# Keeping one over the norms in PSUM, and a second buffer for the rotary product, in the local-attention transformers

## The chip, the core and the metric

The program runs on one core of one Trainium2 chip. The metric is the device time of one execution in microseconds. Three executions of the kernel before took 4264.73, 4267.34 and 4271.99 us, so their median is 4267.34 us. Engines are called PE (matrix), DVE (vector), ACT (scalar activations), POOL (GpSimd) and SP (the queue that issues most transfers).

## The reference, cut to what matters

The whole computation is a chain of four stages. Each stage normalises `x`, runs one branch `s` and one branch `g`, and adds `s * silu(g)` to `x`. The change touches two of the `g` branches: stacks of local-attention transformer layers, one of six layers (16 heads, window 32) and one of two layers (8 heads, window 64). What is computed there for queries and keys is:

```python
def l2norm(t):
    return t / jnp.maximum(jnp.linalg.norm(t, axis=-1, keepdims=True), 1e-12)

qkv = x @ Wqkv
q, k, v = jnp.split(qkv, 3, -1)
q = l2norm(q) * qs
k = l2norm(k) * ksc
q = q * cos * scale + rotate_half(q) * sin * scale
k = k * cos * inv + rotate_half(k) * sin * inv      # inv = 1.0 / scale
out = local_attention(q, k, v)
return out @ Wo
```

Rotation and scaling commute with the division by the norm, so the kernel rotates first and divides last.

## The kernel before, in words

Everything is float32 with channels on the 128 partitions and the 512 positions of one batch on the free axis; there are four batches. The first 1600 us are three earlier stages. Then `transformer("l2")` runs from about 1600 us to 3640 us of the profiled execution, a recurrence follows, and `transformer("l3")` runs from about 3790 us to 4180 us.

In a transformer, a row is one layer of one batch. A row of l2 is cut into two halves of its heads, so l2 has 24 rows and 48 slots, and l3 has 8 rows and 8 slots. `merge` interleaves three Python generators within a slot by weights written by hand:

- `queries_keys` makes the queries and keys of one slot. For queries (i = 0) and keys (i = 1) and for two groups g it runs two projections on PE into a PSUM tile `S`, squares them on ACT (L1287, tile `sqp`), adds the two halves of the squares on POOL (L1288), multiplies the projections by the cosine table on DVE (L1289, into `l_rot`) and by the sine table on DVE (L1291, into `rotp`), and adds the two on POOL (L1292, into `l_rot`).
- `unit_length`, called once for the queries and once for the keys of a slot (96 calls in l2, 16 in l3), sums the squares over the channels with two matmuls of 128x512 into another `S` tile. ACT makes one over the norm out of it in two steps, the logarithm (L1312) and the exponential of minus half of it (L1313), into an SBUF tile `rn`. DVE then multiplies `l_rot` by it in two instructions of 128x1024 (L1316), one for each group. Eight transfers issued on SP's queue (L1323) move the result into the layout of attention (`l_qk`).
- `attention` works on the slot before: values (L1344 copies them out of PSUM, L1346 and L1348 move them), scores (L1377 on PE, L1387, L1391, L1396, L1398 for the softmax), transposes (L1412, L1461) and the output product.
- `feed_forward` of an older row is spread over two slots in l2. In the text, a slot of kind A holds its layer norm (matmuls with `hb,l_k` and `ffg,core`, ACT L1515, L1519, L1520), and a slot of kind B its three gelu tiles (matmuls with `hb,l_w`, ACT L1532, DVE L1534).

[...]A transformer's pool `ps` has three buffers of two banks for all tiles named `S`, and its pool `pm` two of one bank for the tiles named `M`. Projections, sums of squares, values, scores, transposes and feed-forward tiles all take their `S` tile from those three buffers. SBUF tiles of `unit_length` and `queries_keys` come from the pool `t`: `rn` and `rotp` have one buffer each, `sqp` three, `l_rot` two.

The order of the instructions on each engine, and which of the three PSUM buffers a tile gets, are not written by hand: a scheduler decides both when the program is built, from the generators' order and its own durations. The order on each engine is then fixed. A tile that is held longer thus changes which buffers other tiles get.

Of the kernel before, what the change touches and what calls it, by code (L numbers as in the profile page):

```python
# [16 lines left out]
F32 = mybir.dt.float32  # L17
BF16 = mybir.dt.bfloat16
AF = mybir.ActivationFunctionType
ALU = mybir.AluOpType  # L20
# [4 lines left out]
B, S, D = 4, 512, 128  # L25
# [1143 lines left out]
class _Transformer:  # L1169
# [93 lines left out]
    def queries_keys(self, rows):  # L1263


        net, nc, W = self.net, self.nc, self.W
        for l, b in rows:
            hb = net.shifted(net.tok(self.y, b), self.TP, 3)

            hk = hb.rearrange("p (u s k) -> p s u k", s=2, k=W)  # L1270
            for gp in range(self.GP):
                w = self.part("qk", l, gp)
                before = None
                made = []
                for i in range(2):
                    tab = self.tables(l, i)
                    t = self.TP.tile([128, 2, 2, S], F32, name=self.pre + "_rot", bufs=2)
                    sums = []
                    for g in range(2):
                        p = self.S2()  # L1280
                        for h in range(2):
                            c = 128 * (4 * g + 2 * i + h)
                            o = p[:, h, :]
                            net.mm(o.rearrange("p (s u k) -> p s u k", s=2, k=W) if i else o, w[:, c : c + 128], hk if i else hb)
                            yield 0.86
                        sq = self.TP.tile([128, 2, S], F32, name="sqp", bufs=3)
                        nc.scalar.activation(sq, p, AF.Square)  # L1287
                        nc.gpsimd.tensor_tensor(sq[:, 0, :], sq[:, 0, :], sq[:, 1, :], ALU.add)  # L1288
                        nc.vector.tensor_tensor(t[:, g], p, tab[:, 0], ALU.mult)  # L1289
                        m = self.TP.tile([128, 2, S], F32, name="rotp", bufs=1)  # L1290
                        nc.vector.tensor_tensor(m, p, tab[:, 1], ALU.mult)  # L1291
                        nc.gpsimd.tensor_tensor(t[:, g], t[:, g], m[:, ::-1, :], ALU.add)  # L1292
                        sums.append(sq)
                        if before:
                            made.append((yield from self.unit_length(*before)))
                            before = None
                    before = sums, t
                made.append((yield from self.unit_length(*before)))
                self.made[l, b, gp] = hb, made
                yield None  # L1300

    def unit_length(self, sums, t):

        net, nc = self.net, self.nc
        p = self.S2()
        for g in range(2):
            net.mm(p[:, g, :], self.ones, sums[g][:, 0, :])
            yield 0.86  # L1310
        rn = self.TP.tile([128, 2, S], F32, name="rn", bufs=1)
        nc.scalar.activation(rn, p, AF.Ln, bias=self.tiny)  # L1312
        nc.scalar.activation(rn, rn, AF.Exp, scale=-0.5)  # L1313
        for g in range(2):

            nc.vector.scalar_tensor_tensor(  # L1316
                t[:, g], rn[:, g, :].unsqueeze(1).to_broadcast([128, 2, S]), 1e12, t[:, g], ALU.min, ALU.mult
            )
        out = self.QK.tile([128, 2, 2, S], F32, name=self.pre + "_qk")
        for r in range(4):  # L1320
            for h in range(2):
                x = 32 * (2 * (r % 2) + h)
                nc.sync.dma_start(out[x : x + 32, :, r // 2, :], t[32 * r : 32 * r + 32, :, h, :])  # L1323
        return out
# [365 lines left out]
```

## Time and the profile before

| | |
|---|---|
| median of three runs | 4267.34 us (4264.73 to 4271.99) |
| the profiled execution, its own time | 4258.36 us |
| its span, first to last instruction | 4256.7 us |
| mean granted clock of PE | 0.927 |
| PE busy in l2 (1600 to 3640 us) | 1737.69 of 2040 us |
| DVE busy in l2 | 1435.78 us |
| ACT busy in l2 | 918.42 us |
| POOL busy in l2 | 742.16 us |
| L1316, 224 instructions, whole program | 366.2 us busy, mean 1672 ns |

A row of the profile names the line of the kernel, the engine, the operation, and the tiles as output <- inputs. The tile names `l2_rot` and `l3_rot` are both shown as `l_rot`. "Idle before" is the time that an engine stood idle before such an instruction, and the name behind the arrow is what ended that idle time. Busy shares are averages; what a change in one instruction is worth depends on who waits for it.

### The profile page before, as it was taken

The numbers are of one execution on the slowest core, as the hardware profiler recorded it, in microseconds if no ns is written. First come the engines' busy times: TensorE is split into PE (matmuls) and PEld (weight loads), VectorE is DVE, ScalarE is ACT, GpSimd is POOL, SyncE is SP. The second block draws the span as 40 slices with busy tenths as digits, with TensorE's granted clock in tenths as the row PEclk, the third lists the DMA queues.
The fourth block names the chain that finished last, engine by engine and source line by source line (L and its number), as shares of the span: only waits on it lengthen the run. The fifth ranks groups of instructions, "written<-read, shape, count | busy, mean of one in ns | idle before, by whom it ended". The sixth has DMA issues, their size and how long they took to land.

```text
span 4256.7 us, 105246 instructions
## 1 busy us (share of the span) xinstructions
PE 3632.9 (85%) x46765; PEld 1894.8 (45%) x46891; DVE 2521.8 (59%) x3429; ACT 1832.3 (43%) x2495; POOL 1200.4 (28%) x994
## 2 busy tenths in 40 slices
PE   7887999898999986888888888888888888768888
PEld 4554555344444433444444444444444444334444
DVE  6665555205433516677677777777667676447775
ACT  3344666331333343444444444444444444424554
POOL 1011444100111224333333433343333333033221
PEclk7678999996989988999999999999999999879999
DMA  1000000000000004334233424333333332222221
GB/s 35 7 24 26 1 1 1 28 10 7 1 3 2 1 15 113 85 81 106 70 89 98 95 67 120 70 86 94 86 73 92 87 85 69 75 85 68 58 63 43
DMA packets 123574, 236.11 MB, mean 55 GB/s; under 512 B 29625, under 2 KB 44129, under 8 KB 117729
## 3 DMA queue, kind: packets, MB, share of 16 engines
q1 hardware_dynamic: 114064, 209.58, 20.3%
q10 hardware_dynamic: 8624, 19.29, 1.4%
q8 instruction: 369, 6.05, 0.6%
q0 software_dynamic: 432, 0.51, 0.1%
q14 instruction: 85, 0.69, 0.1%
HBM read 50.08 MB, written 5.54 MB: 13 GB/s over the span
## 4 chain that ended last, share of the span: by engine, by line
PE 53%; DVE 16%; ACT 16%; issue 8%; POOL 3%; DMA 3%; SPq 1%; DVEq 0%; POOLq 0%; ACTq 0%
PE S L122 29%; PE M L122 8%; PE S L126 4%; PE S L1377 3%; PE o L1092 3%; DVE l_rot L1316 3%; DVE rotp L1291 3%; ACT l_P L581 3%; DVE l_rot L1289 2%; ACT l_PT L1412 2%; PE o L614 2%; ACT rn L1312 2%; POOL l_rot L1292 2%; ACT sqp L1287 1%; ACT l_P L1396 1%
## 5 line engine op out<-in xcount | busy, mean ns | idle before, releaser
L1292 POOL TENSOR_TENSOR l_rot<-l_rot,rotp 128x1024 f32<-128x1024 f32 x224 | 533.3, 2381 | 459.1 <-DVE rotp L1291 421.6
L1288 POOL TENSOR_TENSOR sqp<-sqp 128x512 f32<-128x512 f32 x224 | 315.6, 1410 | 1010.2 <-ACT sqp L1287 1009.6
L122 PE MATMUL S<-hb,l_wqk 128*128 128x512 f32 x896 | 501.4, 659 | 108.4 <-ACT l_vo L1344 32.3
L1287 ACT ACTIVATE sqp<-S 128x1024 f32<-128x1024 f32 x224 | 229.3, 1024 | 411.0 <-PE S L122 408.6
L1316 DVE SCALAR_TENSOR_TENSOR l_rot<-rn,l_rot 128x1024 f32<-128x1024 f32 x224 | 366.2, 1672 | 64.8 <-ACT rn L1313 62.3
L1289 DVE TENSOR_TENSOR l_rot<-S,l_tab 128x1024 f32<-128x1024 f32 x224 | 272.9, 1218 | 163.7 <-ACT sqp L1287 161.8
L126 PE MATMUL S<-core,l_P 128*128 128x128 f32 x1856 | 269.5, 288 | 57.3 <-DVE rotp L1291 13.5
L122 PE MATMUL S<-l_KT,l_QT 32*128 32x256 f32 (+7 forms) x1536 | 261.9, 505 | 34.8 <-ACT l_P L1114 14.2
L126 PEld LDWEIGHTS S<-core,l_P 128*128 128x128 f32 x1856 | 211.3, 146 | 177.2 <-issue 67.4
L1291 DVE TENSOR_TENSOR rotp<-S,l_tab 128x1024 f32<-128x1024 f32 x224 | 271.6, 1213 | 22.0 <-POOL l_rot L1292 21.8
L122 PE MATMUL S<-sqp,l_k 128*128 128x512 f32 x448 | 241.7, 633 | 33.3 <-POOL sqp L1288 24.9
L1114 ACT ACTIVATE l_P<-S 128x1024 f32<-128x1024 f32 x160 | 156.7, 1022 | 254.6 <-PE S L122 254.5
L1377 PE MATMUL S<-l_qk 64*32 64x64 f32 (+1 forms) x13312 | 222.1, 236 | 43.3 <-issue 34.3
L122 PEld LDWEIGHTS S<-hb,l_wqk 128*128 128x128 f32 x896 | 150.1, 199 | 244.0 <-issue 102.2
L122 PE MATMUL S<-l_wv,hb 128*64 128x256 f32 (+1 forms) x1600 | 237.1, 403 | 7.8 <-ACT rn L1312 2.4
L1377 PEld LDWEIGHTS S<-l_qk 64*32 64x32 f32 (+1 forms) x13312 | 174.1, 110 | 154.5 <-issue 151.0
L1412 ACT COPY l_PT<-S 128x1024 f32<-128x1024 f32 x128 | 129.5, 1012 | 250.1 <-PE S L126 250.0
L1067 DVE TENSOR_REDUCE l_mx<-S 128x2 f32<-128x768 f32 (+1 forms) x192 | 154.9, 863 | 134.1 <-PE S L1006 134.1
L1398 DVE TENSOR_REDUCE rs<-l_P 128x16 f32<-128x1024 f32 (+1 forms) x128 | 155.8, 1217 | 124.2 <-ACT l_P L1396 124.1
L122 PE MATMUL M<-l_OT,l_wo 128*128 128x512 f32 (+1 forms) x512 | 222.7, 546 | 4.1 <-ACT l_OT L1461 2.2
L1118 POOL TENSOR_SCALAR_AFFINE_SELECT l_P<-l_P 128x256 f32<-128x256 f32 x256 | 99.4, 406 | 409.9 <-ACT l_P L1114 405.1
L1387 DVE TENSOR_REDUCE mx<-S 128x16 f32<-128x1024 f32 (+1 forms) x128 | 155.7, 1217 | 98.7 <-PE S L1377 98.5
(359 smaller groups left out, 6619.9 us busy)
## 6 DMA issues: line engine op xcount, KB each, us to landing
l_qk<-l_rot SPq DMA_DIRECT2D x896, 128.0 KB
l_ve<-l_vo SPq DMA_DIRECT2D x112, 256.0 KB
l_ve<-l_vo SPq DMA_DIRECT2D x96, 224.0 KB
l_tab<-in_k_rot_l ACTq DMA_DIRECT2D x16, 1024.0 KB
l_wqk<-in_l2Wqkv SPq DMA_DIRECT2D x12, 512.0 KB
l_wv<-in_l2Wqkv SPq DMA_DIRECT2D x12, 256.0 KB
l_wo<-in_l2Wo SPq DMA_DIRECT2D x12, 256.0 KB
l_ve<-l_vo SPq DMA_DIRECT2D x24, 128.0 KB
```

What stands on the lines that cost most here:

```text
L122: self.nc.tensor.matmul(out, lhsT, rhs, start=start, stop=stop)
L126: self.nc.tensor.transpose(out, in_, self.ident[:n, :n])
L1114: nc.scalar.activation(P[u], s[u], AF.Exp, scale=scale)
L1287: nc.scalar.activation(sq, p, AF.Square)
L1288: nc.gpsimd.tensor_tensor(sq[:, 0, :], sq[:, 0, :], sq[:, 1, :], ALU.add)
L1289: nc.vector.tensor_tensor(t[:, g], p, tab[:, 0], ALU.mult)
L1291: nc.vector.tensor_tensor(m, p, tab[:, 1], ALU.mult)
L1292: nc.gpsimd.tensor_tensor(t[:, g], t[:, g], m[:, ::-1, :], ALU.add)
L1316: nc.vector.scalar_tensor_tensor(t[:, g], rn[:, g, :].unsqueeze(1).to_broadcast([128, 2, S]), 1e12, t[:, g], ALU.min, ALU.mult)
L1377: net.nc.tensor.matmul(sv[W * bl : W * bl + W, e, t, g, :].rearrange("p (s k) -> p s k", s=2), qk[0][r, g, j, W * c : W * c + W], kw, star ...
L1398: nc.vector.tensor_reduce(rs, P.rearrange("p t g e k -> p (t g e) k"), axis=AX.X, op=ALU.add)
L1412: self.nc.scalar.copy(u["PT"], t)
```

## The change

The tile `rn` is gone. The logarithm and the exponential are written back into the PSUM tile `p` that holds the sums of squares, and the two divisions on DVE read one over the norms there. So this `S` tile is given back after the second division instead of after the logarithm. The tile `rotp` gets a second buffer in SBUF; it is as large as `rn` was, 4 KB in each partition.

```diff
-                        m = self.TP.tile([128, 2, S], F32, name="rotp", bufs=1)
+                        m = self.TP.tile([128, 2, S], F32, name="rotp", bufs=2)
...
-        rn = self.TP.tile([128, 2, S], F32, name="rn", bufs=1)
-        nc.scalar.activation(rn, p, AF.Ln, bias=self.tiny)
-        nc.scalar.activation(rn, rn, AF.Exp, scale=-0.5)
+        nc.scalar.activation(p, p, AF.Ln, bias=self.tiny)
+        nc.scalar.activation(p, p, AF.Exp, scale=-0.5)
         for g in range(2):
 
             nc.vector.scalar_tensor_tensor(
-                t[:, g], rn[:, g, :].unsqueeze(1).to_broadcast([128, 2, S]), 1e12, t[:, g], ALU.min, ALU.mult
+                t[:, g], p[:, g, :].unsqueeze(1).to_broadcast([128, 2, S]), 1e12, t[:, g], ALU.min, ALU.mult
             )
```

No instruction is added or taken away. Line numbers behind L1310 are lower by one after the change.

## The prediction

> **What bounds the kernel now.** I read the page's engine rows first, then the stretch of l2 alone, then the lines that change, then who PE waits for, then one slot in order of time.
>
> ```profile
> 1600.00:3640.00 2040.00, 1737.69 (x29203) 888.16 (x29296) 1435.78 (x1528) 918.42 (x1034) 742.16 (x434) 0.97 0.36 87
> ```
> The columns are PE, PE's weight loads, DVE, ACT, POOL, clock, DMA share and GB/s. In l2, PE is busy 85% of the time and stands idle for 302 us. Those 302 us are nearly all that a faster DVE can buy there. l3 (3790 to 4180 us) has 63 us of PE idle time.
>
> ```profile
> L1288 POOL TENSOR_TENSOR sqp<-sqp 128x512 f32<-128x512 f32 x224 | 315.6, 1410 | 1010.2 <-ACT sqp L1287 1009.6
> L1316 DVE SCALAR_TENSOR_TENSOR l_rot<-rn,l_rot 128x1024 f32<-128x1024 f32 x224 | 366.2, 1672 | 64.8 <-ACT rn L1313 62.3
> ```
> The page's groups: count, then busy us and mean ns of one, then idle time before. L1316's instructions one by one, beside two others of their size (shortest, median, longest ns):
> ```profile
> L1316 DVE SCALAR_TENSOR_TENSOR l_rot<-rn,l_rot x224: 1207/1226/3368, 1622.9 to 4175.8; 128x1024 f32<-128x1024 f32 x112
> L1289 DVE TENSOR_TENSOR l_rot<-S,l_tab x224: 1171/1223/1226, 1610.6 to 4168.5; 128x1024 f32<-128x1024 f32 x112
> L1291 DVE TENSOR_TENSOR rotp<-S,l_tab x224: 1172/1214/1226, 1611.7 to 4170.9; 128x1024 f32<-128x1024 f32 x112
> ```
> The size is equal and the operands differ: L1289 and L1291 read one operand in PSUM and are never longer than 1226 ns; L1316 reads two in SBUF and reaches 3368 ns.
>
> ```profile
> PE S L122 <- issue: 60.6, 37, 4.5
> PE S L126 <- ACT l_PT L1412: 45.1, 44, 1.1
> PE S L122 <- DVE rotp L1291: 42.5, 40, 7.1
> PE S L122 <- ACT l_vo L1344: 36.7, 47, 1.1
> PE S L1377 <- issue: 30.5, 38, 4.1
> PE S L126 <- DVE rotp L1291: 23.4, 31, 5.0
> ...
> PE S L122 <- ACT rn L1312: 1.4, 2, 1.2
> ```
> These are PE's waits in l2: total us, times, longest. 66 us end with L1291, which stands behind L1316 in DVE's queue. Only 1.4 us end with the logarithm L1312, which releases the sums' buffer today.
>
> ```profile
> 2513.47 1.21 DVE L1291 TENSOR_TENSOR rotp<-S,l_tab 128x1024 f32<-128x1024 f32 x1
> 2515.91 4.50 DVE L1316 SCALAR_TENSOR_TENSOR l_rot<-rn,l_rot 128x1024 f32<-128x1024 f32 x2 [1.22 <-ACT rn L1313]
> 2521.22 0.69 DVE L1521 TENSOR_TENSOR hb<-S,ffu 128x512 f32<-128x512 f32 x1 [0.81 <-ACT ffu L1520]
> ...
> 2514.77 2.35 POOL L1292 TENSOR_TENSOR l_rot<-l_rot,rotp 128x1024 f32<-128x1024 f32 x1 [2.31 <-DVE rotp L1291]
> 2517.08 2.25 POOL L1288 TENSOR_TENSOR sqp<-sqp 128x512 f32<-128x512 f32 x1
> ```
> One slot of kind A in order of time (start, us). While POOL works, two divisions take 4.50 us and POOL's add 2.25; alone (2505.14) the pair took 2.36, and L1288's usual time is 1.27. Over l2 the pairs span 2.45 and 4.42 us (queries, keys of kind A) and 3.48 and 3.22 (kind B).
>
> **The change part by part.**
>
> *Divisions.* 224 at 1226 in place of 1672 ns free 100 us of DVE; L1288 at its median 1272 in place of 1410 frees 31 us of POOL. No row shows this instruction with an operand in PSUM. Bounds: 1223 ns (L1289) and 1672 (still stretched); I take 1223. [...]
>
> *Logarithm and exponential.* 112 of each as before. No row writes PSUM from ACT. Bounds for the exponential: 1022 ns (L1114, PSUM to SBUF, the nearest), and 2.1 us if reading and writing one bank took turns (twice 1058). I take 1.06 us: 0.
>
> *The buffer held longer.* Before, a sums' tile is held from its first matmul to the end of L1312, 4.86 us in the median; to the end of the second division of the same call it would be 10.2. With the old choice of buffers, the next tile in that buffer starts before that division's end in 74 of 96 calls of l2 and 12 of 16 of l3, by 318 and 48 us in sum. [...]But the changed program's order shows that the scheduler hands buffers out anew. PE's work (0.86 us for each 128x512 product, 0.11 for a 128x256 one, 0.03 for a small one, as spaced in the trace) between the sums and the next tile of that buffer is then 7.2 or 9.7 us for the queries (next are the keys' sums), and for the keys 2.6 in kind A (next is `hb,l_k`) and 4.3 in kind B (`hb,l_w`). Needed are 1.11 + 1.06 + 2.35 and four hand-overs of 0.04 to 0.1, about 4.75. So queries wait for nothing, and kind A's keys stall PE by 2.1 us.
>
> *What that stall is worth* I walk through in the slot above, in the changed order. Keys' sums end 2513.63, logarithm 2514.78, exponential 2515.87, divisions 2518.25 instead of 2520.41. PE: projections to 2515.66, eight value products to 2516.5, then the stall; `hb,l_k` 2518.3 to 2519.3; eight value products to 2520.2; `ffg,core` to 2521.15. ACT copies the values by 2521.3, and the masks, at 2521.96 before, start at 2521.3: before, PE stood waiting there for ACT's copies anyway. Behind the divisions on DVE are now the two copies L89 and L90, which wait for those value products, then L1289 and L1291, done 2523.5 (before 2524.99). The next projections need that buffer: 2523.5 (before 2522.92). Transposes L126 of `l_P` 2524.5 (before 2525.05), of `l_On` 2526.6 (before 2527.62). Scores follow, and behind them `mx` L1387, earlier by 2 us if PE's stream doesn't stall as it did before (2.46 us, "issue", at 2530.4 to 2533.03), by about 0.5 if it does. I take 1.2 us gained for kind A. The same walk through kind B (2541 to 2583 us): `hb,l_w` now waits for a value copy in its own buffer (2559.2 instead of 2557.01), the three gelu tiles end 2564.7 (before 2564.9), masks 2566.25 (before 2566.74), transposes of `l_On` about 2571 (before 2572.37), values held by L1291 at 2574.4 (before 2574.94): 0.5 us gained.
>
> *SP and transfers.* Eight transfers of `l_qk` start with the divisions' end, so 2.2 us sooner in kind A; PE waits for them 0.4 us in all, and POOL's L1292 35.8 us in 14 places, off the path: 0. The transfers of the values queue behind them on SP; were those on the path, up to 2 us more for each slot of kind A.
>
> *Second `rotp`.* L1291 waited 21.8 us for POOL's add in 22 places. Gain between 0 and 21.8; part lies in the walk, so 5 more. It lets POOL fall behind by one add; POOL is busy 36%, which hides it.
>
> *Sum.* 22 pairs of slots at 1.7: -37. Four slots of l2 without feed-forward have 3.4 us of cover against 4.75: +4. l3: cover 4.8 for the keys, but there the division starts 2.46 us behind the logarithm, so 5.9 are needed: 8 x 1.2 = +9. `rotp` -5. Total -29, say -30: the profiled execution, 4258.36 us, becomes 4228. It stands 9 us under the median of 4267.34; the forecast for the median is 4237.
>
> **The rivals.**
>
> *DVE is the limit more than the walk shows.* All the stretch comes off the path: 2.0 + 1.1 + 0.8 us for each pair, 24 pairs, -94; 4173. For: 66 us of PE wait end with L1291. Against: much of PE's waiting is ACT's copies and "issue", which stay.
>
> *PE's own stream decides.* The stalls named "issue" (60.6 + 30.5 us, no cause shown) and ACT's copies absorb what DVE gains: 0; 4267.
>
> *Slower: the held buffer binds.* Place: the third tile after the keys' sums, `hb,l_k` in kind A and `hb,l_w` in kind B. Price: 4.75 less the cover, 2.15 + 0.45, if nothing behind it comes back: 24 x 2.6 = 62, with l3 +71, less 10 for `rotp`; 4328. With a part recovered, 4300. It decides from the point where the stall is more than the 2 us by which the divisions shorten, for instance where other DVE work stands in front of them or the exponential takes over 2 us.
>
> *It doesn't do what it says.* The division stays stretched in PSUM too: the walk's 2520.45 in place of 2518.25 turns kind A into +1.5; 24 x 1.5 = 36; 4303. Against: 448 rows of L1289 and L1291 with no stretch.
>
> **How the numbers follow.** The forecast -30 has 0.45 (its own range 4207 to 4259), the large gain 0.17, nothing 0.12, the held buffer 0.21, the stretch that stays 0.05. A measurement of this kernel tells about 0.2%, 8.5 us, from no change. Faster: 0.45 + 0.17 = 0.62; same 0.12; slower 0.26. The range 4182 to 4312 leaves out half of the large gain and the worse half of the held buffer.
>
> **What the changed profile would show.** Right: L1315 (the division) at 1223 ns with no long ones, 275 us in all; L1288 near 1272; the exponential's row (L1312 then) at 1.02 to 1.12 us; L1291 no longer waiting for POOL; a new wait of PE on L1315 of about 2 us in every second slot of l2; PE's waits on L1291 down from 66 us. Wrong: L1315 with a longest time over 2 us, an exponential near 2 us, PE's waits on L1315 over 100 us in sum, or PE's waits in l2 not smaller than 302 us.

## The result, and the profile after

The changed kernel took 4201.92 us in the median of 4 runs (4199.46 to 4212.01). The kernel before took 4266.03 us beside it (4259.58 to 4271.99). The ratio is 0.9854, with a 95% interval of 0.9833 to 0.9876: 64 us less, where 30 us less was forecast. The profiled executions are 55 us apart (4203.18 against 4258.36 us), since that of the kernel before was 8 us under its median; the sums below are made against these 55.

The first view is the table of busy time in a stretch of l2. Columns are PE, PE's weight loads, DVE, ACT, POOL, granted clock, DMA share and GB/s.

```profile
1600.00:3600.00 2000.00, 1721.69 (x29476) 896.95 (x29571) 1368.06 (x1536) 913.36 (x1036) 711.34 (x434) 0.98 0.37 91
```

PE is busy in 86% of this stretch instead of 85, and DVE in 68% instead of 70. PE therefore still has idle time of 278 us in 2000. The kernel did not come to the end of what PE can give.

Next the rows of the instructions that change. The first two are groups of the page (count, busy us, mean ns, idle before), the others rows of single lines (shortest, median and longest ns), the last two of them of the kernel before:

```profile
L1315 DVE SCALAR_TENSOR_TENSOR l_rot<-S,l_rot 128x1024 f32<-128x1024 f32 x224 | 267.1, 1220 | 86.4 <-ACT S L1312 76.6
L1288 POOL TENSOR_TENSOR sqp<-sqp 128x512 f32<-128x512 f32 x224 | 287.4, 1283 | 856.8 <-ACT sqp L1287 856.5
L1315 DVE SCALAR_TENSOR_TENSOR l_rot<-S,l_rot x224: 1206/1223/1226, 1627.8 to 4123.1; 128x1024 f32<-128x1024 f32 x112
L1311 ACT ACTIVATE S<-S,l_tiny x112: 1068/1088/1097, 1623.1 to 4119.8; 128x1024 f32<-128x1024 f32 x112
L1312 ACT ACTIVATE S<-S x112: 1008/1008/1046, 1624.2 to 4120.9; 128x1024 f32<-128x1024 f32 x112
```
```profile
L1312 ACT ACTIVATE rn<-S,l_tiny x112: 1096/1114/1138, 1616.8 to 4172.5; 128x1024 f32<-128x1024 f32 x112
L1313 ACT ACTIVATE rn<-rn x112: 1055/1058/1088, 1617.9 to 4173.6; 128x1024 f32<-128x1024 f32 x112
```

The division's longest time fell from 3368 to 1226 ns and its mean from 1672 to 1220. POOL's L1288 came down with it, from 1410 to 1283. The logarithm and the exponential, now both in place in PSUM, are 26 and 50 ns shorter, not longer.

PE's waits in the same stretch of l2 (total us, times, longest):

```profile
PE S L122 <- DVE rotp L1291: 76.4, 77, 7.2
PE S L122 <- ACT l_vo L1343: 41.6, 52, 1.1
PE S L122 <- issue: 28.2, 31, 2.1
PE S L1376 <- issue: 23.4, 32, 4.2
PE S L122 <- DVE l_rot L1315: 21.0, 21, 1.0
PE S L126 <- DVE rotp L1291: 15.8, 33, 2.4
...
PE S L126 <- ACT l_PT L1411: 11.3, 43, 1.1
```

The new wait is the row on L1315: 21 times 1.0 us, once for nearly every slot of kind A. Gone are 34 us on `l_PT`, and 32 us of the "issue" before L122. Waits on L1291 had been forecast to fall; they went from 66 to 92 us.

Measured from logarithm to logarithm, the time went as follows (queries' logarithm of a slot to that of the next, one profiled execution each; a steady slot is the mean of 21 or 22, and single ones lie up to 5 us from it):

| part | before | after | difference |
|---|---|---|---|
| up to l2's first logarithm | 1616.8 | 1623.1 | +6.3 |
| l2, first four slots (no feed-forward) | 165.3 | 151.4 | -13.9 |
| l2, one steady slot of kind B | 42.30 | 40.91 | -1.39 |
| l2, one steady slot of kind A | 42.96 | 42.41 | -0.55 |
| l2, all 48 slots | 2010.7 | 1954.6 | -56.1 |
| between l2's last and l3's first logarithm | 169.0 | 166.6 | -2.4 |
| l3, first to last logarithm | 376.0 | 375.5 | -0.5 |
| after l3's last logarithm | 84.2 | 81.7 | -2.5 |

The parts sum to the 55 us. The 6.3 us at the start go with one wait of PE for the weights of the first projection, 6.8 us.

### The profile page after: what moved, and what is told of

Same layout as the page of the kernel before. It is cut to its first block, busy times and chain, and to the rows that moved or that the text cites. A ratio compares the mean times of both kernels' runs of the same rounds, so it can differ in the third digit from the quotient of the medians.

```text
span 4201.5 us, 105470 instructions
## 1 busy us (share of the span) xinstructions
PE 3603.6 (86%) x46765; PEld 1896.5 (45%) x46891; DVE 2439.9 (58%) x3429; ACT 1824.6 (43%) x2495; POOL 1166.3 (28%) x994
## 4 chain that ended last, share of the span: by engine, by line
PE 50%; DVE 20%; ACT 16%; issue 7%; DMA 3%; POOL 3%; SPq 1%; DVEq 0%; POOLq 0%; ACTq 0%
PE S L122 27%; PE M L122 8%; PE S L126 4%; DVE l_rot L1289 4%; DVE rotp L1291 4%; PE o L1092 3%; ACT l_P L581 3%; ACT sqp L1287 2%; DVE l_rot L1315 2%; PE S L1376 2%; PE o L614 2%; ACT l_PT L1411 1%; ACT l_vo L1343 1%; POOL l_rot L1292 1%; ACT l_P L1395 1%
## 5 line engine op out<-in xcount | busy, mean ns | idle before, releaser
L1292 POOL TENSOR_TENSOR l_rot<-l_rot,rotp 128x1024 f32<-128x1024 f32 x224 | 532.6, 2379 | 417.3 <-DVE rotp L1291 395.2
L122 PE MATMUL S<-hb,l_wqk 128*128 128x512 f32 x896 | 489.0, 646 | 93.0 <-DVE rotp L1291 39.0
L1288 POOL TENSOR_TENSOR sqp<-sqp 128x512 f32<-128x512 f32 x224 | 287.4, 1283 | 856.8 <-ACT sqp L1287 856.5
L1289 DVE TENSOR_TENSOR l_rot<-S,l_tab 128x1024 f32<-128x1024 f32 x224 | 272.9, 1218 | 216.7 <-ACT sqp L1287 215.1
L1287 ACT ACTIVATE sqp<-S 128x1024 f32<-128x1024 f32 x224 | 229.7, 1025 | 298.3 <-PE S L122 286.3
L1315 DVE SCALAR_TENSOR_TENSOR l_rot<-S,l_rot 128x1024 f32<-128x1024 f32 x224 | 267.1, 1220 | 86.4 <-ACT S L1312 76.6
L122 PE MATMUL S<-l_KT,l_QT 32*128 32x256 f32 (+7 forms) x1536 | 261.9, 505 | 34.8 <-ACT l_P L1114 14.2
L122 PE MATMUL S<-sqp,l_k 128*128 128x512 f32 x448 | 243.2, 635 | 35.4 <-POOL sqp L1288 24.9
L1291 DVE TENSOR_TENSOR rotp<-S,l_tab 128x1024 f32<-128x1024 f32 x224 | 271.6, 1212 | 0.0
L1114 ACT ACTIVATE l_P<-S 128x1024 f32<-128x1024 f32 x160 | 156.7, 1022 | 254.8 <-PE S L122 254.5
L122 PEld LDWEIGHTS S<-hb,l_wqk 128*128 128x128 f32 x896 | 150.4, 197 | 220.1 <-issue 84.5
L122 PE MATMUL S<-l_wv,hb 128*64 128x256 f32 (+1 forms) x1600 | 221.9, 397 | 3.5 <-DVE rotp L1291 2.1
L122 PE MATMUL M<-l_OT,l_wo 128*128 128x512 f32 (+1 forms) x512 | 220.2, 545 | 3.9 <-ACT l_OT L1460 2.3
L1311 ACT ACTIVATE S<-S,l_tiny 128x1024 f32<-128x1024 f32 x112 | 122.1, 1090 | 205.0 <-PE S L122 200.5
```

The lines of the kernel that those rows point to most:

```text
L122: self.nc.tensor.matmul(out, lhsT, rhs, start=start, stop=stop)
L1114: nc.scalar.activation(P[u], s[u], AF.Exp, scale=scale)
L1315: nc.vector.scalar_tensor_tensor(t[:, g], p[:, g, :].unsqueeze(1).to_broadcast([128, 2, S]), 1e12, t[:, g], ALU.min, ALU.mult)
```

## The experiments

Two theories were set against each other first. One says that the gain comes from the divisions, which are no longer stretched while POOL works, and that the longer hold of the sums' tile costs little because the divisions are short. The other says that the gain comes from elsewhere: the second `rotp`, ACT's steps in PSUM, or buffers handed out anew.

### The second rotary buffer alone

```diff
-                        m = self.TP.tile([128, 2, S], F32, name="rotp", bufs=1)
+                        m = self.TP.tile([128, 2, S], F32, name="rotp", bufs=2)
```

> The kernel before with two buffers for rotp, and nothing else. Theory S (the gain of 64 us is the stretch of L1316 that leaves with its second SBUF operand): the second buffer takes away only L1291's waits on POOL, 21.8 us in all, much of it off the path, so 0 to 12 us faster, 4254 to 4266; L1316 keeps its mean near 1672 ns. Theory R (the second rotp buffer brings the gain, by letting DVE run ahead): 40 us or more faster.

It took 4254.07 us, ratio 0.9973 (0.9957 to 0.9988): 12 us less, at the edge of what the first theory allowed. The instructions of DVE, ACT and POOL follow one another in the trace as in the kernel before, so the buffer brought no new order there. Nearly all of the gain lies in the first four slots of l2 (165.3 to 155.0 us); the steady slots are the same to 0.1 us (42.23 and 42.90). This agrees with a row of the kernel before, DVE's waits from 1600 to 1790 us:

```profile
DVE rotp L1291 <- POOL l_rot L1292: 11.1, 5, 2.5
```

Half of the 21.8 us that L1291 waited for POOL lay in these four slots, and PE waits there most for L1291 itself: 29.5 us of some 49 us of waits from 1600 to 1790 us. In the steady slots the other half was hidden.

### The PSUM part alone

The change with `rotp` at one buffer.

> The changed kernel with one buffer for rotp. Theory S: keeps nearly all of the gain, 4200 to 4215, L1315 at 1220 ns, L1291 waits for POOL by some 20 us again. Theory R: loses most of it, 4240 or more.

It took 4216.1 us, ratio 0.9889 (0.9867 to 0.9910): 50 us less, one us above the range that the first theory gave. With the 12 to 13 us of the run above this makes nearly the 64 of the whole change. The steady slots (40.89 and 42.42) are those of the whole change, and so is the order of the instructions on DVE, ACT and POOL.

### The hold alone, with divisions from SBUF

The kernel before, with a product of one column behind the second division that reads the sums' tile and so keeps it:

```diff
+        kept = net.stat(1, "kept")
+        nc.vector.tensor_tensor(kept, p[:, 1, 0:1], t[:, 1, 0, 0:1], ALU.mult)
```

> The kernel before (rn in SBUF, one rotp buffer) with the tile of the sums kept until after the second division, by a DVE product of one element for each of 112 calls that reads both; about 0.1 us each, 10 us of DVE in all. Theory S: the hold alone costs, since divisions stay stretched: in kind A the tile comes free about 3 us later than PE is there for it; 20 to 70 us slower than before, 4285 to 4335. If the hold were free with the buffers handed out anew: within 10 us of before. If handing the buffers out anew were itself what gains: faster than before by 20 us or more.

It took 4341.4 us, ratio 1.0178 (1.0152 to 1.0204): 75 us more, beyond the 20 to 70 expected. Slots of kind A take 46.33 us, 3.4 more than before; kind B is unchanged (42.39). PE's waits, and one slot of kind A on DVE in order of time (start, us):

```profile
PE S L122 <- DVE kept L1320: 94.9, 46, 4.6
```
```profile
2552.49 4.51 DVE L1316 SCALAR_TENSOR_TENSOR l_rot<-rn,l_rot 128x1024 f32<-128x1024 f32 x2 [1.22 <-ACT rn L1313]
2557.10 0.16 DVE L1320 TENSOR_TENSOR kept<-S,l_rot 128x1 f32<-128x1 f32 x1
```

The pair of divisions is the stretched one (4.51 us), and PE waits up to 4.6 us for the tile. This is the held buffer that the prediction feared. Its price there, 71 us before the gain from `rotp`, is near the 75, but it had been worked out for short divisions. In this kernel the hold is longer by the tiny product too, which the next run prices.

### The same hold, with divisions from PSUM

The change with one `rotp`, and with the same `kept` product behind the divisions.

> The change without the second rotary buffer, and with the same tiny product behind the second division that the run of the held buffer alone had. It separates the hold from the stretch: both kernels hold the sums' tile to the same point behind the second division, but here the divisions read PSUM. If the 75 us lost by the hold alone come from the stretched divisions that lengthen it, this run is near the change without the second buffer (4216): 4210 to 4230, with PE waiting some 20 to 35 us for the tiny product. If they come from the tiny product and its order in DVE's queue, 4290 to 4340.

It took 4222.86 us, ratio 0.9888 (0.9871 to 0.9905). Against the same kernel without the tiny product (4216.1) that is 7 us more, so the product and the later release that comes with it cost about that. The last two kernels hold the tile to the same point of the code and differ in where ACT writes and what the divisions read; they lie 118 us apart. ACT's two steps, shorter by 26 and 50 ns in 112 calls, are 9 us of that in sum. Nor is it the order that the scheduler chose: in the two traces DVE's instructions follow one another alike through the whole of l2, and part only in l3 (ACT's differ in places). PE's wait here is a ninth of that above, and less than the 20 to 35 us expected:

```profile
PE S L122 <- DVE kept L1319: 10.8, 9, 3.0
```

So the same hold loses 75 us if the divisions are stretched, and leaves a gain if they are short. That the divisions are short decides the sign of the whole change. The hold is not free with short ones either, as the `M` tiles below show.

### ACT writes to PSUM, divisions still from SBUF

The logarithm in place in PSUM, the exponential from PSUM into an SBUF tile `rn`; the tile is given back after the exponential.

```diff
-        nc.scalar.activation(rn, p, AF.Ln, bias=self.tiny)
-        nc.scalar.activation(rn, rn, AF.Exp, scale=-0.5)
+        nc.scalar.activation(p, p, AF.Ln, bias=self.tiny)
+        nc.scalar.activation(rn, p, AF.Exp, scale=-0.5)
```

> The logarithm stays in PSUM, the exponential reads it there and writes rn to SBUF, the divisions read two SBUF operands as before; one rotp buffer. The tile of the sums is held about 1.1 us longer. Theory S: the ACT part of the change alone; the two ACT steps took 1088 + 1008 ns in the changed kernel against 1114 + 1058, so at most 8 us gained, less what the longer hold costs: 4255 to 4285. Theory A (the cheaper ACT steps, which stand in front of every division, carry a good part of the gain): 20 us or more faster.

It took 4245.37 us, ratio 0.9948 (0.9933 to 0.9963): 21 us less, although the divisions stay as stretched as ever (mean 1710 ns). That is outside the range of theory S and reaches the 20 us of theory A, of which ACT's own steps give only a part. The exponential:

```profile
L1313 ACT ACTIVATE rn<-S x112: 1018/1025/1052, 1623.7 to 4162.3; 128x1024 f32<-128x1024 f32 x112
```

ACT's two steps are 25 and 33 ns shorter in the median, 6 us in all 112 pairs. The order of the instructions on DVE and ACT is no longer that of the kernel before, and kind A falls by 0.8 us while kind B rises by 0.3; that the other 15 us come from this order and the buffers handed out anew is likely, but not shown. This also says that a part of the 50 us of the PSUM part need not come from the divisions.

### Without the feed-forward

Both kernels with the feed-forward of the transformers left out, to see a slot where PE has less to do.

> The kernel before, with the feed-forward pass of both transformers left out (that part of the computation is missing). A reference for the next run; about 3680 to 3850 us, since some 36 PE products of 128x512 fall away in each slot of l2.

> The changed kernel, with the feed-forward pass of both transformers left out as in the run before (that part of the computation is missing). The first four slots of l2, which have no feed-forward, became 3.5 us shorter each; 48 slots of that kind give 130 to 170 us less than the run before it. If the cover of such slots is the 3.4 us of the prediction and binds, each loses 1 us: 50 us more than the run before. If the first four gained for being first (a pipeline that fills), the difference is 20 to 60 us.

They took 4095.92 us (ratio to the kernel before 0.9589, 0.9566 to 0.9611) and 3966.77 us (0.9283, 0.9260 to 0.9307). The first expectation was far off: leaving out this work of PE saved only 174 us (the kernel before took 4270.34 us beside it). It rested on a miscount too, since the pass has 11 products of 128x512 in two slots, some 5 us of PE in each slot at the 0.86 us a product of the prediction, and not 36 in each. The second was met but for one us: 129 us between the two. Slots (steady, kind B and kind A) and waits of PE from 1640 to 3400 us, before and after the change:

| | kind B | kind A |
|---|---|---|
| before, with feed-forward | 42.30 | 42.96 |
| before, without | 41.26 | 42.04 |
| after, with feed-forward | 40.91 | 42.41 |
| after, without | 37.96 | 39.13 |

```profile
PE S L126 <- DVE rotp L1289: 215.3, 80, 6.2
PE S L122 <- DVE rotp L1289: 50.9, 42, 5.2
```
```profile
PE S L126 <- DVE rotp L1289: 100.7, 72, 2.4
PE S L122 <- ACT l_vo L1341: 76.5, 81, 1.1
...
PE S L122 <- DVE rotp L1289: 17.2, 44, 2.9
```

(L1289 here is the sine product, L1291 elsewhere.) In the kernel before, the feed-forward cost 1.0 us in a slot: a slot was as long as DVE's chain made it, and PE did the feed-forward while it would have waited. Without it PE waits 266 us for the sine product, of 385 us in which it is idle. After the change DVE's chain allows slots of 38 to 39 us, 3 us shorter, and the feed-forward costs 3 us. So the change is worth 3 us in a slot, and about 2 of them are taken back by the work that DVE's slowness had hidden. What sets the length of a slot of the whole changed kernel is not shown by this: PE is busy in 86% of it, and its longest waits are still those on L1291 (92 us). One caution: PE's granted clock in these stretches was 0.91 without the change and 0.95 with it; what that did to the length of PE's work was not shown.

### The layer norm away from the held buffer

The whole change, and the two products of the feed-forward's layer norm in `M` tiles instead of an `S` tile, so that `hb,l_k` no longer waits for the second division:

```diff
-            p = self.S2()
-            net.mm(p[:, 0, :], self.cen, hb)
+            p = self.M()
+            net.mm(p, self.cen, hb)
...
-            net.mm(p[:, 1, :], net.mean, sq)
+            v = self.M()
+            net.mm(v, net.mean, sq)
```

> The whole change, and besides it the two products of the feed-forward's layer norm go to tiles named M in place of the tile S that waits for the division. If the held buffer costs what PE waits for it (21 times 1.0 us on L1315 in kind A), the waits vanish and each pair of slots loses about 1 us: 22 us less than the changed kernel, about 4180. If kind A's gain is small for another reason (the stretched affine step of the layer norm, values copied late), the time stays at 4196 to 4206 though the waits are gone. If the M tiles are themselves awaited (value products use them), 4210 or more.

It took 4170.92 us, ratio 0.9763 (0.9744 to 0.9781), some 31 us less than the change as it is, where 22 were expected. PE's waits in l2:

```profile
PE S L122 <- ACT l_vo L1343: 50.7, 63, 1.1
PE S L122 <- issue: 39.9, 37, 3.2
PE S L122 <- DVE rotp L1291: 35.6, 45, 7.4
...
PE S L122 <- DVE l_rot L1315: 2.3, 1, 2.3
```

The waits on L1315 are gone but for one, and kind A falls by 0.68 us to 41.73; kind B is 0.18 longer. Compared with the kernel before, both kinds now gain the same, 1.2 us. So kind A's smaller share in the change was the stall: 1.0 us of waiting cost about 0.7. But l2's steady slots give only some 11 of the 31 us. The larger part is in l3, where first to last logarithm fell from 375.5 to 352.4 us, and which no expectation had named; 7 of these 23 us come back behind l3 (81.7 to 88.7 us). In the changed kernel PE waited there for the product that ends the layer norm's own hold of an `S` tile (3740 to 4170 us):

```profile
PE S L126 <- DVE hb L1520: 10.8, 5, 2.2
```

This row is absent with the `M` tiles. What else shortened l3 was not taken apart.

### The affine step of the layer norm on ACT

With the `M` tiles a second thing had gone away, a stretch of L1521 (last section). To tell it from the buffer, the changed kernel got this step on ACT, once with the `S` tile and once with the `M` tiles:

```diff
-            nc.vector.tensor_scalar(hb, hb, self.col(l, 0), self.col(l, 1), ALU.mult, ALU.add)
+            nc.scalar.activation(hb, hb, AF.Identity, bias=self.col(l, 1), scale=self.col(l, 0))
```

> The whole change, with the affine step of the feed-forward's layer norm (hb times one column plus another, stretched from 532 to 2133 ns in 24 rows of the changed kernel) on ACT in place of DVE; the layer norm's products keep their S tile. It tells whether the 31 us that the M tiles brought came from the buffer or from this step, which was back at 532 ns there. If the stretched step costs time, 4165 to 4185 (24 times 1.6 us on DVE is at most 38 us). If it is off the path and the buffer was the cause, 4195 to 4205. If ACT is the nearer limit (its copies of the values are waited for 42 us already), 4205 to 4220.

> M tiles for the layer norm's products and the affine step on ACT together. The step is not stretched once the M tiles are used, so it saves DVE 24 times 0.53 us, 13 us of an engine that is not the bound, and gives ACT some 0.5 us each: 4165 to 4176, no different from M tiles alone (4171). If ACT's queue is the nearer limit, 4180 or more.

With the `S` tile it took 4190.42 us, ratio 0.9831 (0.9812 to 0.9851). This lies between two of the expected ranges, and the intervals do not tell it apart from the change itself (0.9854). The trace tells more: in l2, where the stretched rows are, all 48 slots take 1954.0 us against 1954.6, so the stretched step costs nothing there. Half of the 12 us by which this run is shorter lie in front of l2's first logarithm (1616.7 against 1623.1 us), where PE did not wait for the first projection's weights. With the `M` tiles it took 4165.8 us, 0.9771 (0.9748 to 0.9793), no different from the `M` tiles alone. These two runs have the step on ACT alike and were taken beside the same kernel before; they are 25 us apart. So the buffer is the cause of nearly all of those 31 us.

## Why the prediction was right or wrong, point by point

The forecast (faster, by 30 us) had the right sign and was right on the divisions; the measured gain is twice as large.

*The step that failed.* It is the sum's treatment of the stretches outside the steady slots. The four slots of l2 without feed-forward stood there at +4, with -5 for `rotp`, and l3 at +9: the held buffer was charged, and the shorter divisions were given nothing, without a reason. The runs showed -13.9 us for those four slots and -0.5 us for l3, which is 22 of the 26 us by which the sum fell short. In those four slots PE does not wait for the division once, the PSUM part alone takes 5.1 us off them and the second `rotp` alone 10.3; in l3 PE waits for the division once, for 1.3 us. (A slip beside it: 3.4 us of cover against 4.75 makes 5.4 us in four slots, not 4.)

*The divisions.* Right in full: 1223 ns in the median, 267 us in all (275 forecast), none long, L1288 at 1283 (1272 forecast). So the stretch did leave with the second SBUF operand: the pair at 2496.57 us took 2.56 us beside L1292 and L1288 on POOL (2.36 and 1.27 us), where the pair of the walked slot took 4.50 beside the same two (2.35 and 2.25 us). Nor did reading PSUM make the division longer: 1226 ns from SBUF and 1223 from PSUM in the median, 1207 and 1206 for the shortest.

*Logarithm and exponential.* Taken at no change, inside bounds of 1022 to 2100 ns. They became 26 and 50 ns shorter. Small, and on the safe side.

*The hold.* "About 4.75 us" needed from the sums' end to the second division's end was right (4.76 in kind A), and the overruns of 318 and 48 us that the old choice of buffers would have had did not come: PE waited 21 us for the division in l2 and 1.3 us in l3. Wrong was the cover of the keys' tile. It was put at 2.6 us from "0.11 for a 128x256 one". But the eight value products show two records each:

```profile
2494.44 1.95 PE L122 MATMUL S<-hb,l_wqk 128*128 128x512 f32 x4
2496.33 1.95 PE L122 MATMUL S<-l_wv,hb 128*64 128x256 f32 x16
2499.27 1.10 PE L122 MATMUL S<-hb,l_k 128*128 128x512 f32 x2 [0.99 <-DVE l_rot L1315]
```

Sixteen records in 1.95 us are 0.24 us for a product, twice the term of the sum. From the end of the sums (2494.37) to the end of the value products (2498.28) is 3.9 us, so the stall is 0.99 and not 2.1 us. This error did not make the forecast too small: eight more value products stand between the stall and the masks, and half of their time was missing too.

*l3.* The sum had +9 for a stall of 1.2 us in each of 8 slots. There value products are 128x512, so the unit price has no part in it. What was needed came out at 5.3 us in the mean and not 5.9, because the divisions start sooner behind the logarithm (1.2 us instead of 2.5), and PE waited for L1315 once. Why the cover sufficed where 5.8 us were needed (four of the eight slots) was not taken apart.

*The second `rotp`.* The sum had -5; alone it gave 12 us, 10.3 of them in the four slots without feed-forward. This term was mis-sized because the 21.8 us of waits were looked at as one sum. Split by place, 11.1 us lay in those four slots, where PE mostly waits for DVE, and there almost all of it counted.

*The steady slots.* Forecast -1.2 for kind A and -0.5 for kind B, -37 in all; measured -0.55 and -1.39, about -42. The sum is near by luck, since the parts are exchanged. The following is in medians over the slots, counted from the queries' logarithm. In kind A the walk has the masks 0.7 us earlier than before; in the trace they come 0.7 us later, most of it by the second group of value products, which takes 1.95 us where the walk had 0.9; and kind A still pays about 0.7 us for its stall, as the `M` tiles showed. In kind B the walk holds almost to its end: PE now waits 1.11 us for the value copy before the first `hb,l_w` in 21 of 22 slots, that product starts 2.05 us later (2.2 in the walk), the masks come 0.4 us earlier (0.5), and the transposes of `l_On` 1.6 us earlier (1.4). There the walk let the values' wait for L1291 take the gain back to 0.5 us. In the trace the 1.6 us last to the end of the slot.

*The rivals.* "DVE is the limit more than the walk shows" was nearer the truth for the kernel before than its chance of 0.17: without feed-forward each slot gains 3 us. With it about 2 of them are taken back, which points to "PE's own stream decides", though its waits named "issue" fell from 91 to 52 us. "The held buffer binds" was priced right in kind: the hold with stretched divisions loses 75 us, and the point from which it decides, divisions that do not shorten, is what the two kernels with the `kept` product show. "The stretch stays", at 4303, was priced too low as far as the nearest run tells: the hold with stretched divisions from SBUF took 4341, with one `rotp` and the `kept` product.

*The sum again.* The profiled executions differ by 55 us and the sum by 29. Of the missing 26, the four slots without feed-forward give 13 (-13.9 where the hold and `rotp` together had -1), l3 9.5, the steady slots 5, the stretches between and behind the transformers 5, and the late weights at l2's start take 6 back.

*What stays open.* How the 50 us of the PSUM part divide between the divisions, ACT's steps and buffers handed out anew is not additive: ACT's write to PSUM alone gives 21, and the same hold with and without the stretch differs by 118. Open too are the 15 us of that run which ACT's shorter steps do not explain, and what else shortened l3 with the `M` tiles.

## What to carry to other kernels

The same hold went with 75 us more where the divisions stayed stretched and with 47 us less where they were short, so price a longer hold together with the length of the work that holds it, and compare the time needed with the time covered. Take the unit price of every kind of product from its own row, with all its records counted; here one product priced at half its time made a stall twice as long as it is, and the work behind it half as long. Where a stage is charged with a change's cost, credit it with the change's gain as well. And split a sum of waits by stage before giving it a share: the waits in the four slots where PE mostly waited for DVE were worth nearly their full time, those in the other 44 next to nothing.

## What the runs showed of the hardware beyond that

ACT in place in PSUM was not slower than from PSUM to SBUF or from SBUF to SBUF: 128x1024 exponentials took 1058 ns (SBUF to SBUF), 1025 (PSUM to SBUF) and 1008 (PSUM to PSUM) in the median, logarithms 1114 (PSUM to SBUF) and 1088 (in place).

The stretch under POOL's work moved to another instruction. L1521 reads and writes SBUF alone; in the kernel before it was L1522, and none of its 23 rows in l2 ran beside an add of POOL: beside 17 of them POOL did the memset of one column, L88 (0.82 to 0.83 us in 16 of them), beside six nothing. Rows of l2, before and after the change:

```profile
L1522 DVE TENSOR_SCALAR hb<-hb,l_cols x23: 530/532/547, 1760.8 to 3636.4; 128x512 f32<-128x512 f32 x23
```
```profile
L1521 DVE TENSOR_SCALAR hb<-hb,l_cols x24: 531/2133/2142, 1754.3 to 3628.4; 128x512 f32<-128x512 f32 x24
```
```profile
2505.43 0.68 DVE L1520 TENSOR_TENSOR hb<-S,ffu 128x512 f32<-128x512 f32 x1
2506.15 2.13 DVE L1521 TENSOR_SCALAR hb<-hb,l_cols 128x512 f32<-128x512 f32 x1
...
2505.65 2.35 POOL L1292 TENSOR_TENSOR l_rot<-l_rot,rotp 128x1024 f32<-128x1024 f32 x1 [2.90 <-DVE rotp L1291]
```

In 15 of the 24 rows DVE's step starts 0.5 us after POOL's add and takes 2.13 instead of 0.53 us; it ends within 0.3 us of it, as if it had waited for it, while POOL's add is not longer for it (2.35 us against a mean of 2379 ns). The other nine take 0.53 to 0.55 us; four of them start before POOL's add, five run with no work of POOL beside them. This instruction reads one large operand, so here a stretch came (2133 ns in the median) without two large operands in SBUF. In the division one such operand left no stretch (1226 ns at the longest). PE hardly waited for it (2.8 us in l2), and moving it to ACT (813 ns there) changed l2's slots by less than one us.

PE's granted clock was not higher in the kernel with less PE work: 0.892 over the whole run of the kernel before without feed-forward, 0.927 with it.
